# One layer's scan over 64 positions: one long scan instruction with reset columns, or sixteen short ones

## The chip, the cores and the metric

The kernel runs on one core of one Trainium2 chip. The metric is the device time of one launch in microseconds (us). Five engines work beside each other, each through its own queue of instructions in a fixed order: TensorE (PE, matmuls), VectorE (DVE), ScalarE (ACT), GpSimd (POOL) and SyncE (SP, which issues nearly all transfers here). An instruction whose operands are not ready stops everything behind it in its engine's queue.

## The reference, cut to what matters

A tensor of 32 images, 512 channels, 32 x 32 positions goes through four residual layers: x = x + layer(groupnorm(x)). Layer 0 weights channels by a spectrum, layer 1 is a grouped 3 x 3 convolution, layer 3 a deformable channel attention. Layer 2 is a three-level state-space model, and it is most of the work. At each level a feature map with 256 channels is read as a sequence of length L = 1024, 256 or 64, once forward and once backward, with 16 states per channel:

```python
dA  = jnp.exp(delta[..., None] * A)
dBx = delta[..., None] * Bs[:, :, None, :] * xt[..., None]
def step(h, inp):
    da, dbx, c = inp
    h = h * da + dbx
    return (h, jnp.einsum('bdn,bn->bd', h, c))
_, ys = lax.scan(step, h0, ...)          # h0 = 0
```

So each of the 256 x 16 pairs of channel and state has its own recurrence over the L positions, which starts from zero. At L = 64 and L = 256 both directions use the same weights and so the same dA and dBx; only the order of the positions differs. The output of a level is layer-normalised and added, doubled in both directions, to the next finer one.

## The kernel before, in words

**Tiles.** A tile for a scan has 128 partitions: 32 channels times 4 states. Its 1024 columns hold one sequence of 1024 positions (level "fine"), or four sequences of 256 (four groups of 32 channels, `nk` = 1), or sixteen sequences of 64 (four groups of channels times four groups of states, `nk` = 4). The function `fine` handles the level of 1024, the function `both` the levels of 256 and 64, with both directions in one call.

**One step of `both`.** PE spreads B over the partitions into PSUM (`pb`, L1548 at 64 positions, L1541 at 256). DVE multiplies it with delta times x (L1555). At 64 positions POOL forms the product delta times A (L1565) and ACT takes the exponential of all 1024 columns (L1580); at 256, ACT does both in four instructions (L1587). DVE scans (L1339 in the helper `scan`, called for r = 0 forward and r = 1 backward), POOL multiplies the result with C (L1625), PE sums over the states (L1635). An image has two halves of channels (d = 0, 1), so at 64 positions there are two exponentials, four scan steps (d, r) and four multiplications on POOL; in 32 images 64, 128 and 128.

**How sixteen sequences share one scan.** At 64 positions the scan instruction runs over all 1024 columns at once. So that no state passes from one sequence to the next, the factor dA in the first column of each sequence has to be zero. A tile `sv` (two buffers, cleared once at the start, L401) serves for this: ACT saves the first columns of `da` in `sv` (L1595) and overwrites them in `da` with zeros (L1599); the forward scan follows; before the backward scan one DVE reduction (L1606) puts the saved first columns back and zeros into the last ones. At 256 positions each of the four sequences already has a scan instruction of its own.

**The order of the work.** Every operation is recorded with an engine, an expected duration, its buffers and a key, a due time. `Plan.order` then replays the recording with the written durations: on each engine it starts, of the operations that are ready and have buffers, the one with the smallest key. What comes out is the instruction order of every engine; the chip only follows it. Keys count 100 units for an image. They are made of the constants at the head of the file: a place in the image for each stage (`FRONT`, `INPUTS`, `LOWER` and so on), shifts by image number (`PHASE`, `FIRST`, `FINAL`), and leads of single operations over their scan (the names ending in `_AHEAD`). `PE_RATE` multiplies the expected duration of every PE operation. Buffers are rings: `da` has 2, `pb` 2, `h` 6, `dt` 4.

**Fillers.** Where the replay leaves PE a gap of over 0.3 us while an accumulator (`y0`, `y1b`) is open, `between` puts matmuls of zeros into it (L1960), 0.8 of the gap by the written unit. `O_AHEAD` sets how early the accumulators are opened (L1364). These fillers add zero, and are real PE work.

Of the kernel before, what the change touches and what calls it, by code (L numbers as in the profile page):

```python
# [8 lines left out]
F32 = mybir.dt.float32  # L9
BF16 = mybir.dt.bfloat16  # L10
AF = mybir.ActivationFunctionType
ALU = mybir.AluOpType

P = 128
# [14 lines left out]
GROUP = 4  # L29
UNITS = 84  # L30

FRONT = (26.98339, 66.33591)
INPUTS = (97.00668, 120.78633)
Z = (73.71537, 86.62189)
DOWN = 115.11838
LOWER = (12.88324, 31.62883)
FINE1 = (22.72857, 46.22736)
FINE0 = (49.76984, 76.03085)
OUTPUT = (111.60985, 122.08898)
BACK = (68.71162, 156.12354)  # L40
SPECTRA = (57.12973, 128.4)

Z_0 = -72.5918
DOWN_0 = -124.07672
LOWER_0 = (-42.64059, -49.8751)
FRONT_E = (47.56605, -25.53413)
INPUTS_E = 6.96675
LOWER_E = (28.33012, 26.10135)
EVACUATE = 122.43595
LN_LATE = 10.7188  # L50
B_AHEAD, A_AHEAD, L_AHEAD, DB_AHEAD = 5.41553, 5.18574, 14.39657, 1.31239
C_AHEAD, Y_AHEAD, F_AHEAD, E_AHEAD = 5.20433, 0.75794, 9.0321, 4.34074
CC_AHEAD, CL_AHEAD, CA_AHEAD, CP_AHEAD = 7.94514, 17.86118, 5.24806, 5.3979
CB_AHEAD, CD_AHEAD = 5.83962, 1.9145
PE_RATE = 0.91418
O_AHEAD = 14.25035


class Buf:
# [175 lines left out]
def between(order):  # L235
# [21 lines left out]
KEEP_MIN, KEEP_SHARE, KEEP_UNIT = 0.3, 0.8, 0.213  # L257
STAGES = ("FRONT", "INPUTS", "DOWN", "LOWER", "FINE1", "FINE0", "OUTPUT", "BACK", "SPECTRA", "WEIGHTS")
PHASE = {
    "FRONT": (1.73998, -0.70898, 2.43732, -0.46783),  # L260
    "INPUTS": (-0.34062, 3.48827, 7.42205, -0.7684),
    "DOWN": (-0.28454, -1.33532, -2.28645, 10.95771),
    "LOWER": (-4.21848, 4.12408, 4.547, 2.27219),
    "FINE1": (-4.94045, -6.76105, 4.24822, 8.46924),
    "FINE0": (1.01816, -1.50111, 1.92083, 9.0252),
    "OUTPUT": (-3.45079, 6.79797, -9.49065, 1.76105),
    "BACK": (2.71819, 0.18102, 6.35319, -8.65591),
    "SPECTRA": (0.07386, 2.29523, -2.67145, -0.1361),
    "WEIGHTS": (4.55431, 2.37816, -5.2352, -47.942),
}  # L270
FIRST = {
    "FRONT": (-29.02061, -15.58957, -4.59773, 10.57713, -17.5828, -1.10449, -1.89262, -0.79223, 1.77484, 0.04765),
    "INPUTS": (5.35602, 0.39704, -1.54139, -3.11792, 3.98507, -25.36453, -4.27892, -2.71805, -3.56424, -9.18247),
    "DOWN": (-18.15189, -3.37029, 10.3643, -17.2826, -7.72621, 2.2188),
    "LOWER": (15.04982, 7.33067, 0.38748, -32.74476, -1.53709, 23.9531),
    "FINE1": (-27.62561, 15.94068, 40.70755, 4.75357, -13.35547, -3.68556),
    "FINE0": (-6.26626, -4.07582, 6.02046, -24.18655, 15.14066, -24.66011),
    "OUTPUT": (0.91761, 10.28771, 13.93866, -20.22127, -6.40573, 7.16333, -28.29682, -3.02744),
    "BACK": (-4.97178, 23.91988, 26.10169, 50.03687, -23.23641, 9.05568, -3.72902, 3.44514),
    "SPECTRA": (-36.87069, -17.04888, -4.24826, -12.25783, 7.70159, 8.04977, 2.40985, -5.14477, 4.98738, -5.21155, -0.54739, -3.88386, 0.27824, -2.0242),  # L280
    "WEIGHTS": (33.69103, -28.68007, 55.07658, 8.03152, 17.55966, 20.12364, -26.01811, -30.12737, -3.71784, 3.05174, 43.2247, -27.22466, -3.82396, -0.9483),
}
FINAL = {
    "FRONT": (-0.73596, -24.67755, -6.33942),
    "INPUTS": (-4.79937, 4.31975, 19.83127),
    "DOWN": (-5.09233, 3.22121, 21.47571),
    "LOWER": (-36.96369, 38.20998, 11.9625),
    "FINE1": (9.75884, -9.86524, 57.70702),
    "FINE0": (6.03965, 18.64503, -9.54717),
    "OUTPUT": (18.40436, -3.78191, 3.95094),  # L290
    "BACK": (49.74549, 3.63925, 12.96738),
    "SPECTRA": (2.96786, -20.64168, 8.41789),
    "WEIGHTS": (-20.80319, 27.97236, -51.95186),
}
T_DMA = 0.42
T_TABLE = 1.3
# [21 lines left out]
def kernel(ctx: ExitStack, tc: tile.TileContext, t: dict, out: bass.AP):  # L318
    nc = tc.nc
# [29 lines left out]
        "sbm": ([96, 256], BF16, 1, True),  # L349
        "sbc": ([96, 64], BF16, 1, True),  # L350
        "dg": ([P, P], F32, 1, True),
        "sv": ([P, 16, 2], F32, 2, True),
        "dt": ([P, 2, HW], F32, 4, True),
        "cb": ([P, HW], F32, 2, True),
        "da": ([P, HW], F32, 2, True),
# [41 lines left out]
    tiles = {}  # L397
    for n, (shape, dt, count, _) in shapes.items():
        tiles[n] = [const.tile(shape, dt, name=f"{n}{i}") for i in range(count)]
    for w in tiles["sv"]:  # L400
        nc.gpsimd.memset(w, 0.0)  # L401

    h_all = const.tile([P, H_TILES * HW], F32, name="h_all")
    tiles["h"] = [h_all[:, i * HW : (i + 1) * HW] for i in range(H_TILES)]
# [26 lines left out]
    for i in (1, 2, 3):  # L431
# [3 lines left out]
        w = const.tile([P, 2, P], F32, name=f"xw{i}")  # L435
        nc.gpsimd.memset(w, 0.0)
        r = slice((0, 80, 112, 120)[i], (0, 80, 112, 120)[i] + RDT)
# [41 lines left out]
    pl = Plan(rings)  # L479
# [19 lines left out]
    def act(fn, n, r, w, key, ptr=False, acq=()):  # L499
        return pl.op("ACT", t_act(n, ptr), fn, r, w, key, acq)  # L500

    def dve(fn, n, r, w, key, acq=()):
        return pl.op("DVE", t_dve(n), fn, r, w, key, acq)
# [833 lines left out]
    def scan(h, da, db, rev):  # L1337
        v = [z[:, ::-1] if rev else z for z in (h, da, db)]
        nc.vector.tensor_tensor_scan(v[0], v[1], v[2], 0.0, ALU.mult, ALU.add)  # L1339
# [156 lines left out]
    def both(lv, f, pre, ysum, below, n, ck):  # L1496
# [4 lines left out]
        nk = HW // (4 * n)  # L1501
# [16 lines left out]
        def pieces(z):  # L1518
            return z.rearrange("p (k q l) -> p k q l", k=nk, q=4)

        o = [P, nk, 4, n]
        for d in range(2):
# [11 lines left out]
            for k0 in range(0, 4, nk):  # L1534
                pb = pl.buf("pb")
# [26 lines left out]
                if nk > 1:  # L1562
# [7 lines left out]
                        ),  # L1570
                        HW, [(dt, 1)], [pr], ck.key(CP_AHEAD),
                    )
                da, sv = pl.buf("da"), nk > 1 and pl.buf("sv")

                def ends(da=da):
                    return pieces(da.t).rearrange("p k q l -> p (k q) l")

                if nk > 1:
                    act(
# [3 lines left out]
                else:  # L1583
                    for q in range(4):
# [5 lines left out]
                            ),  # L1590
                            n, [(dt, 1)], [(da, q)], ck.key(CA_AHEAD), True,
                        )
                if nk > 1:
                    act(
                        lambda sv=sv, ends=ends: nc.scalar.copy(sv.t[:, 0 : 4 * nk, 0:1], ends()[:, :, 0:1]),  # L1595
                        4 * nk, [da], [sv], ck.key(CA_AHEAD),
                    )
                    act(
                        lambda sv=sv, ends=ends: nc.scalar.copy(ends()[:, :, 0:1], sv.t[:, 0 : 4 * nk, 1:2]),  # L1599
                        4 * nk, [sv], [da], ck.key(CA_AHEAD),  # L1600
                    )
                for r in range(2):
                    h = pl.buf("h")
                    if r and nk > 1:
                        dve(
                            lambda sv=sv, ends=ends: nc.vector.tensor_reduce(  # L1606
                                ends()[:, :, 0 : n : n - 1],
                                sv.t[:, 0 : 4 * nk, :].rearrange("p k (e o) -> p k e o", o=1),
                                axis=mybir.AxisListType.X, op=ALU.max,
                            ),  # L1610
                            8 * nk + 60, [sv], [da], ck.key(),
                        )
                    if nk > 1:
                        pl.op(
                            "DVE", 2.21, lambda h=h, da=da, pb=pb, r=r: scan(h.t, da.t, pb.t, r == 1),
                            [da, pb], [h], ck.key(),
                        )
                    else:
                        def scans(h=h, da=da, pb=pb, r=r):
                            for q in range(4):  # L1620
                                scan(*(pieces(z.t)[:, 0, q, :] for z in (h, da, pb)), r == 1)

                        pl.op("DVE", 2.36, scans, [da, pb], [h], ck.key())
                    pool(
                        lambda h=h, k0=k0: nc.gpsimd.tensor_mul(  # L1625
                            pieces(h.t), pieces(h.t),
                            cbv()[:, k0 : k0 + nk, :].rearrange("p k (o l) -> p k o l", o=1).to_broadcast(o),
                        ),
                        HW, [h, cb], [h], ck.key(),
                    )  # L1630

                    def add(h=h, r=r, k0=k0, d=d):
                        for k in range(nk):
                            for q in range(4):
                                nc.tensor.matmul(  # L1635
                                    accv(r)[q * 32 : (q + 1) * 32, d, 0:n], lhsT=sel_y,
                                    rhs=pieces(h.t)[:, k, q, :],
                                    start=False, stop=False,
                                )

                    pe(add, 0.6 if nk == 1 else 0.69, [h], [acc[r]], ck.key(Y_AHEAD))
                    ck.u += 1
# [210 lines left out]
    while b < B:  # L1853
        n = min(1 if b < 2 else 2 if b < 4 else GROUP, B - b)
# [30 lines left out]
    def begin(b):  # L1885
# [4 lines left out]
        if b == 0:  # L1890
            m = moved("FRONT", 0)
            front(b, st[b], -340.0 + m, -310.0 + m)
# [31 lines left out]
    for b in range(B):  # L1924
# [6 lines left out]
        if own:  # L1931
            k = LOWER_E if b else LOWER_0
# [20 lines left out]
    with tc.manual_schedule():  # L1953
        for o in order:
# [3 lines left out]
            n, b, lo = spare.get(o, (0, None, 0))  # L1958
# [96 lines left out]
```

## Time and profile before

| | before |
|---|---|
| median of 3 runs | 10725.92 us (10714.02 to 10737.91) |
| the profiled execution's own time | 10725.94 us |
| its span, first to last instruction | 10723.8 us |
| PE busy | 9886.2 us, 92% (of it fillers L1960: 1478.3 us) |
| DVE busy | 9543.4 us, 89% |
| POOL busy | 8335.1 us, 78% |
| ACT busy | 7440.7 us, 69% |
| transfers | 191 GB/s, 71% of the DMA engines' time |
| granted PE clock | 0.972 |

Busy time counts an engine's overlapped instructions once. A group's "mean" is the length of one instruction from its start to its end, which can be longer than the distance to the next one: where busy time divided by the count is smaller than the mean, instructions overlap. PE's busy time holds the fillers, so that it says little on how near PE is to its limit. "Idle before" is the time an engine stood still just before the instructions of a group.

### The profile page before, as it was taken

The numbers are of one execution on the slowest core, as the hardware profiler recorded it, in microseconds if no ns is written. First come the engines' busy times: TensorE is split into PE (matmuls) and PEld (weight loads), VectorE is DVE, ScalarE is ACT, GpSimd is POOL, SyncE is SP. The second block draws the span as 40 slices with busy tenths as digits, with TensorE's granted clock in tenths as the row PEclk, the third lists the DMA queues.
The fourth block names the chain that finished last, engine by engine and source line by source line (L and its number), as shares of the span: only waits on it lengthen the run. The fifth ranks groups of instructions, "written<-read, shape, count | busy, mean of one in ns | idle before, by whom it ended". The sixth has DMA issues, their size and how long they took to land. (4 is left out here: it accounts for less than half of the span.)

```text
span 10723.8 us, 163029 instructions
## 1 busy us (share of the span) xinstructions
PE 9886.2 (92%) x55995; PEld 4522.1 (42%) x55995; DVE 9543.4 (89%) x9224; ACT 7440.7 (69%) x12932; POOL 8335.1 (78%) x5681
## 2 busy tenths in 40 slices
PE   8999999999999999999999999999999999999987
PEld 5454544434444444344443444434444434333333
DVE  2977878999999999999899998999999999999996
ACT  5677776776777767777777767777677776666654
POOL 2766677788788788887788878888877888878886
PEclk9999999999999999999999999999999999999999
DMA  5677667777877777777777767777777777776654
GB/s 170 163 193 193 178 178 197 193 185 203 217 197 188 196 194 206 210 194 198 193 208 196 199 186 205 197 197 204 196 209 198 189 196 190 202 205 185 166 139 134
DMA packets 897107, 2050.26 MB, mean 191 GB/s; under 512 B 230802, under 2 KB 363178, under 8 KB 883850
## 3 DMA queue, kind: packets, MB, share of 16 engines
q1 hardware_dynamic: 896256, 2039.74, 71.0%
q8 instruction: 442, 7.24, 0.3%
q14 instruction: 391, 3.20, 0.1%
q10 hardware_dynamic: 18, 0.09, 0.0%
HBM read 1609.80 MB, written 429.52 MB: 190 GB/s over the span
## 5 line engine op out<-in xcount | busy, mean ns | idle before, releaser
L1339 DVE TENSOR_TENSOR_SCAN h_all<-da,pb 128x1024 f32<-128x1024 f32 (+1 forms) x4224 | 6125.6, 1493 | 329.5 <-ACT da L1416 118.9
L1430 POOL TENSOR_TENSOR h_all<-h_all,cb 128x1024 f32<-128x1024 f32 x2048 | 4814.8, 2362 | 1582.4 <-DVE h_all L1339 1040.5
L1416 ACT ACTIVATE da<-dt,w_Al 128x1024 f32<-128x1024 f32 x2048 | 2335.9, 1147 | 1480.6 <-DVE h_all L1339 1069.5
L1422 DVE TENSOR_TENSOR pb<-dt,pb 128x1024 f32<-128x1024 f32 x2048 | 2446.1, 1215 | 265.8 <-PE pb L1409 171.7
L1625 POOL TENSOR_TENSOR h_all<-h_all,cb 128x1024 f32<-128x1024 f32 x640 | 1505.7, 2363 | 181.2 <-DVE h_all L1339 103.1
L1409 PE MATMUL pb<-sb,sel_b 96*128 96x512 bf16 x4096 | 1248.5, 387 | 369.6 <-DVE h_all L1339 297.9
L1960 PE MATMUL y<-sel_b,none_b 96*128 96x512 bf16 x5564 | 1478.3, 389 | 5.2 <-DVE sel_b L593 5.2
L1045 PE MATMUL mm<-x,wt 128*128 128x512 f32 x2048 | 981.0, 601 | 17.8 <-ACT x L565 4.0
L1409 PEld LDWEIGHTS <-sel_b 96*128 96x128 bf16 x4096 | 387.3, 102 | 1333.6 <-issue 1253.2
L1960 PEld LDWEIGHTS <-none_b 96*128 96x128 bf16 x5603 | 541.3, 103 | 755.5 <-issue 287.6
L992 PE MATMUL mm<-pk,wk 99*32 99x512 f32 (+1 forms) x6024 | 792.5, 607 | 42.1 <-DMA pk<-in_xp 27.4
L1438 PE MATMUL y<-h_all,w_sel_y 128*32 128x512 f32 x4096 | 615.4, 625 | 1.5 <-POOL h_all L1430 1.4
L710 PE MATMUL mm<-w_dct,sx 128*128 128x128 f32 x3968 | 565.7, 291 | 32.9 <-ACT sx L701 8.0
L710 PEld LDWEIGHTS mm<-w_dct,sx 128*128 128x128 f32 x3968 | 506.2, 199 | 185.7 <-ACT sx L701 42.9
L1438 PE MATMUL y1b<-h_all,w_sel_y 128*32 128x512 f32 x4096 | 569.8, 609 | 0.0
L1045 PEld LDWEIGHTS mm<-x,wt 128*128 128x128 f32 x2048 | 369.7, 189 | 422.1 <-issue 281.1
L1045 PE MATMUL mm<-y,w_out_w 128*128 128x512 f32 x1024 | 514.0, 616 | 15.6 <-ACT g L1715 2.7
L1587 ACT ACTIVATE da<-dt,w_Al 128x256 f32<-128x256 f32 x1024 | 464.0, 503 | 39.5 <-DVE h_all L1339 34.9
L1555 DVE TENSOR_TENSOR pb<-dt,pb 128x1024 f32<-128x1024 f32 x320 | 386.1, 1213 | 72.0 <-PE pb L1541 60.7
L1242 POOL TENSOR_TENSOR g<-g,f 128x512 f32<-128x512 f32 (+2 forms) x384 | 386.7, 1020 | 35.5 <-ACT g L1231 33.5
L1269 PE MATMUL mm<-ln,ones_d 128*128 128x512 f32 (+1 forms) x768 | 392.0, 599 | 20.2 <-ACT f L1075 8.3
L1192 PE MATMUL mm<-xd,dtw 64*128 64x512 f32 (+2 forms) x768 | 363.5, 560 | 35.4 <-DVE xd L1164 7.8
(286 smaller groups left out, 14556.5 us busy)
## 6 DMA issues: line engine op xcount, KB each, us to landing
dt<-dd SPq DMA_DIRECT2D x2048, 256.0 KB, 7.7
pk<-in_xp SPq DMA_DIRECT2D x753, 297.0 KB, 5.8
cb<-cd SPq DMA_DIRECT2D x1536, 128.0 KB, 3.7
dd<-g SPq DMA_DIRECT2D x256, 512.0 KB, 6.4
xr<-x SPq DMA_DIRECT2D x128, 512.0 KB, 6.8
yv<-fs SPq DMA_DIRECT2D x128, 512.0 KB, 5.0
dt<-ddm SPq DMA_DIRECT2D x512, 128.0 KB, 3.4
sx<-in_x SPq DMA_DIRECT2D x124, 512.0 KB, 5.3
```

Of the source, the lines that this page charges most:

```text
L710: nc.tensor.matmul(ps.t[:, j * P : (j + 1) * P], lhsT=sx.t[:, 1, i : i + P], rhs=dct, start=True, stop=True,)
L992: nc.tensor.matmul(ps.t[32 * q : 32 * q + 32, r0 * IMG : r1 * IMG].rearrange("p (r k) -> p r k", k=IMG), lhsT=wk.t[:, q, 32 * dy : 32 * dy ...
L1045: nc.tensor.matmul(ps.t, lhsT=w(k)[:, m * P : (m + 1) * P], rhs=r()[:, cols], start=(k == 0 and not opened), stop=(k == len(rhs) - 1),)
L1339: nc.vector.tensor_tensor_scan(v[0], v[1], v[2], 0.0, ALU.mult, ALU.add)
L1409: nc.tensor.matmul(pb.t[:, cols], lhsT=sel_b[:, k, :], rhs=sb.t[:, cols], start=True, stop=True,)
L1416: lambda da=da, z=dt[q], k=k, g=g: nc.scalar.activation(da.t, z.t[:, 1, :], AF.Exp, scale=A[lv][:, k, g : g + 1]),
L1422: lambda pb=pb, z=dt[q]: nc.vector.tensor_mul(pb.t, z.t[:, 0, :], pb.t), HW,
L1430: lambda h=h, cb=cb: nc.gpsimd.tensor_mul(h.t, h.t, cb.t), HW, [h, cb], [h],
L1438: nc.tensor.matmul(acc[i].t[q * 32 : (q + 1) * 32, :], lhsT=sel_y, rhs=hs[q].t[:, cols], start=False, stop=False,)
L1587: lambda da=da, quads=quads, q=q, g=g, k0=k0: nc.scalar.activation(pieces(da.t)[:, 0, q, :], quads(1)[:, q, :], AF.Exp, scale=A[lv][:, k0, ...
L1625: lambda h=h, k0=k0: nc.gpsimd.tensor_mul(pieces(h.t), pieces(h.t), cbv()[:, k0 : k0 + nk, :].rearrange("p k (o l) -> p k o l", o=1).to_br ...
L1960: nc.tensor.matmul(b.t[:, lo : lo + b.kept], lhsT=none_b, rhs=flat(sel_b)[:, 0 : b.kept], start=False, stop=False)
```

## The change

The tile `sv`, its clearing, the two ACT copies and the DVE reduction are gone. At 64 positions each scan step issues sixteen scan instructions of 64 columns, one for each sequence, where it issued one of 1024; the two scan steps of a half now use the same unchanged `da`. The written duration of the step is 3.15 in place of 2.21. Besides, nearly every constant of the order has another value: all stage places, all shifts by image, all leads, and `PE_RATE`.

```diff
-LOWER = (12.88324, 31.62883)
+LOWER = (13.513, 28.96824)
...
-CC_AHEAD, CL_AHEAD, CA_AHEAD, CP_AHEAD = 7.94514, 17.86118, 5.24806, 5.3979
-CB_AHEAD, CD_AHEAD = 5.83962, 1.9145
-PE_RATE = 0.91418
-O_AHEAD = 14.25035
+CC_AHEAD, CL_AHEAD, CA_AHEAD, CP_AHEAD = 7.47032, 19.39182, 5.02592, 5.90281
+CB_AHEAD, CD_AHEAD = 5.58549, 1.69698
+PE_RATE = 0.87173
+O_AHEAD = 22.13866
...
-        "sv": ([P, 16, 2], F32, 2, True),
...
-    for w in tiles["sv"]:
-        nc.gpsimd.memset(w, 0.0)
...
-                da, sv = pl.buf("da"), nk > 1 and pl.buf("sv")
-
-                def ends(da=da):
-                    return pieces(da.t).rearrange("p k q l -> p (k q) l")
+                da = pl.buf("da")
...
-                if nk > 1:
-                    act(
-                        lambda sv=sv, ends=ends: nc.scalar.copy(sv.t[:, 0 : 4 * nk, 0:1], ends()[:, :, 0:1]),
-                        4 * nk, [da], [sv], ck.key(CA_AHEAD),
-                    )
-                    act(
-                        lambda sv=sv, ends=ends: nc.scalar.copy(ends()[:, :, 0:1], sv.t[:, 0 : 4 * nk, 1:2]),
-                        4 * nk, [sv], [da], ck.key(CA_AHEAD),
-                    )
                 for r in range(2):
                     h = pl.buf("h")
-                    if r and nk > 1:
-                        dve(
-                            lambda sv=sv, ends=ends: nc.vector.tensor_reduce(
-                                ends()[:, :, 0 : n : n - 1],
-                                sv.t[:, 0 : 4 * nk, :].rearrange("p k (e o) -> p k e o", o=1),
-                                axis=mybir.AxisListType.X, op=ALU.max,
-                            ),
-                            8 * nk + 60, [sv], [da], ck.key(),
-                        )
-                    if nk > 1:
-                        pl.op(
-                            "DVE", 2.21, lambda h=h, da=da, pb=pb, r=r: scan(h.t, da.t, pb.t, r == 1),
-                            [da, pb], [h], ck.key(),
-                        )
-                    else:
-                        def scans(h=h, da=da, pb=pb, r=r):
+
+                    def scans(h=h, da=da, pb=pb, r=r):
+                        for k in range(nk):
                             for q in range(4):
-                                scan(*(pieces(z.t)[:, 0, q, :] for z in (h, da, pb)), r == 1)
-
-                        pl.op("DVE", 2.36, scans, [da, pb], [h], ck.key())
+                                scan(*(pieces(z.t)[:, k, q, :] for z in (h, da, pb)), r == 1)
+
+                    pl.op("DVE", 2.36 if nk == 1 else 3.15, scans, [da, pb], [h], ck.key())
```

More of the change, by code (lines that the diff above doesn't have):

```diff
@@ L30 @@
 UNITS = 84
[L32 to L35, printed above, removed]
-LOWER = (12.88324, 31.62883)
[L37 to L52, printed above, removed]
-CC_AHEAD, CL_AHEAD, CA_AHEAD, CP_AHEAD = 7.94514, 17.86118, 5.24806, 5.3979
-CB_AHEAD, CD_AHEAD = 5.83962, 1.9145
-PE_RATE = 0.91418
-O_AHEAD = 14.25035
+FRONT = (27.31004, 67.02807)
+INPUTS = (93.94834, 125.04711)
+Z = (74.67623, 81.77805)
+DOWN = 114.77346
+LOWER = (13.513, 28.96824)
+FINE1 = (23.19548, 47.21091)
+FINE0 = (51.35358, 78.96264)
+OUTPUT = (111.95446, 118.11289)
+BACK = (55.5241, 161.03937)
+SPECTRA = (54.70856, 128.30351)
+Z_0 = -105.07863
+DOWN_0 = -220.95057
+LOWER_0 = (-29.86063, -34.61059)
+FRONT_E = (48.91459, 3.04387)
+INPUTS_E = 9.5435
+LOWER_E = (29.80023, 7.07295)
+EVACUATE = 133.23714
+LN_LATE = 10.8511
+B_AHEAD, A_AHEAD, L_AHEAD, DB_AHEAD = 5.37078, 5.10994, 14.35379, 1.62967
+C_AHEAD, Y_AHEAD, F_AHEAD, E_AHEAD = 6.56594, 0.57586, 8.98335, 5.19642
+CC_AHEAD, CL_AHEAD, CA_AHEAD, CP_AHEAD = 7.47032, 19.39182, 5.02592, 5.90281
+CB_AHEAD, CD_AHEAD = 5.58549, 1.69698
+PE_RATE = 0.87173
+O_AHEAD = 22.13866
 class Buf:
@@ L259 @@
 PHASE = {
[L260 to L269, printed above, removed]
+    "FRONT": (4.73761, -0.28903, 5.77875, -0.61673),
@@ L270 @@
+    "INPUTS": (-5.30511, 2.65734, 5.73485, -0.37277),
+    "DOWN": (6.25453, -0.83769, -3.93846, 12.43911),
+    "LOWER": (-3.28637, 3.5377, 4.35329, 0.76018),
+    "FINE1": (-3.7777, -7.32571, 7.73012, 9.46184),
+    "FINE0": (-2.66305, -5.3351, -1.25818, 7.73328),
+    "OUTPUT": (-1.17514, 4.15285, -0.39845, 1.58054),
+    "BACK": (7.14305, -7.8301, 10.47171, -7.42362),
+    "SPECTRA": (0.05649, 2.36357, -2.74389, -0.17737),
+    "WEIGHTS": (4.03052, -12.29821, -8.33443, -45.10858),
 }
 FIRST = {
-    "FRONT": (-29.02061, -15.58957, -4.59773, 10.57713, -17.5828, -1.10449, -1.89262, -0.79223, 1.77484, 0.04765),
@@ L273 @@
[L273 to L278, printed above, removed]
@@ L279 @@
-    "BACK": (-4.97178, 23.91988, 26.10169, 50.03687, -23.23641, 9.05568, -3.72902, 3.44514),
-    "SPECTRA": (-36.87069, -17.04888, -4.24826, -12.25783, 7.70159, 8.04977, 2.40985, -5.14477, 4.98738, -5.21155, -0.54739, -3.88386, 0.27824, -2.0242),
-    "WEIGHTS": (33.69103, -28.68007, 55.07658, 8.03152, 17.55966, 20.12364, -26.01811, -30.12737, -3.71784, 3.05174, 43.2247, -27.22466, -3.82396, -0.9483),
+    "FRONT": (-27.52564, 11.14284, -15.05171, 30.02941, -23.32033, -15.87875, -12.07511, -2.96433, 0.9052, -2.73885),
@@ new lines @@
+    "INPUTS": (32.98002, 24.43932, 14.72288, 5.28944, -5.64191, -22.2843, -24.62038, -3.24191, -10.37639, -7.01109),
+    "DOWN": (-21.56508, -10.93218, 11.5105, -24.24021, -21.3927, 12.70338),
+    "LOWER": (34.01591, 10.32587, -4.47171, -25.48991, -0.66856, 21.58012),
+    "FINE1": (-32.26982, 15.66706, 32.27702, 7.15662, -39.90577, -0.34393),
+    "FINE0": (-3.26079, -9.71483, 21.02106, -24.35115, 19.72641, -26.05953),
+    "OUTPUT": (5.45725, 12.33286, 15.60198, -35.96714, -5.3198, 6.13576, -12.72858, -2.34173),
@@ L282 @@
+    "BACK": (-10.08665, 8.28069, 39.62304, 42.64832, -26.4346, -13.8819, -30.40457, -0.78097),
+    "SPECTRA": (-50.89355, -28.32336, -14.82804, -14.45231, 31.14369, 15.55765, 5.72886, -2.17973, 35.40677, -21.2843, -0.54779, -0.93164, -1.76293, -3.42053),
+    "WEIGHTS": (32.4412, -30.83669, 71.89057, 8.90844, 26.65968, 4.84071, -42.77211, -78.41173, -6.62991, 12.28345, 64.52262, -31.64528, 0.33291, 7.3203),
 }
 FINAL = {
-    "FRONT": (-0.73596, -24.67755, -6.33942),
-    "INPUTS": (-4.79937, 4.31975, 19.83127),
@@ L286 @@
[L286 to L293, printed above, removed]
+    "FRONT": (27.443, -32.26499, -6.70537),
+    "INPUTS": (-7.67726, -4.99709, 2.73194),
+    "DOWN": (4.51104, -6.37409, 79.88748),
@@ L294 @@
+    "LOWER": (-33.40447, 53.58347, 29.60236),
+    "FINE1": (12.63865, -13.89714, 82.8607),
+    "FINE0": (-5.19006, 1.7855, 9.26835),
+    "OUTPUT": (35.93553, 21.8516, 7.85491),
+    "BACK": (41.20561, -6.17039, 8.64673),
+    "SPECTRA": (-3.41341, -2.3044, 9.3649),
+    "WEIGHTS": (5.14431, 61.44699, -79.7461),
 }
```

## The prediction

> **What bounds the kernel now.** First the groups by line on DVE, with shapes kept apart. Behind the bar stand busy time and the mean length of one; then the idle time just before the group and what ended it.
>
> ```profile
> L1339 DVE TENSOR_TENSOR_SCAN h_all<-da,pb 128x1024 f32<-128x1024 f32 x2176 | 4908.9, 2275 | 326.9 <-ACT da L1416 118.9 <-PE y1b L1438 74.4 <-ACT da L1599 55.5
> L1339 DVE TENSOR_TENSOR_SCAN h_all<-da,pb 128x256 f32<-128x256 f32 x2048 | 1220.4, 661 | 2.6 <-issue 1.1 <-ACT da L1587 0.7
> L1606 DVE TENSOR_REDUCE da<-sv 128x32 f32<-128x32 f32 x64 | 13.2, 207 | 1.3
> ```
>
> Two thirds of DVE's busy time is scans. Of the 2176 long ones, 128 belong to the level of 64, the rest to the finest one. The last name in the first row is a wait that this change bears on: 55.5 us in which a scan waited for the copy that clears first columns.
>
> Then busy time by stretch (us, then PE, PE weight loads, DVE, ACT, POOL, then clock, DMA share, GB/s).
>
> ```profile
> 0.00:150.00 150.00, 124.07 (x778) 86.47 (x779) 20.43 (x82) 64.51 (x169) 21.86 (x64) 0.87 0.67 191
> ...
> 2400.00:5000.00 2600.00, 2413.24 (x13760) 1096.39 (x13760) 2430.01 (x2338) 1888.52 (x3277) 2117.49 (x1434) 0.98 0.75 201
> 5000.00:9800.00 4800.00, 4455.75 (x25218) 2000.26 (x25217) 4447.32 (x4181) 3384.42 (x5821) 3901.66 (x2641) 0.97 0.74 197
> ```
>
> From 2400 us on DVE works 93% of the time, ACT 71 to 73%, POOL 81%. PE's 93% contains the fillers, so DVE is the engine that sets the pace. Over the whole span DVE stands still 10723.8 - 9543.4 = 1180 us: about 206 before 300 us, 313 from there to 2000, 576 from there to 10300, 85 after that. So about 890 us of idle lie in the body, and a DVE microsecond is worth close to one of span.
>
> Third, a stretch with one image's step at 64 positions, on DVE in order of time (start, length).
>
> ```profile
> 4832.78 2.29 DVE L1339 TENSOR_TENSOR_SCAN h_all<-da,pb 128x1024 f32<-128x1024 f32 x1
> 4834.99 0.13 DVE L552 TENSOR_SCALAR sms<-mm 128x1 f32<-128x1 f32 x1
> 4835.11 0.21 DVE L1606 TENSOR_REDUCE da<-sv 128x32 f32<-128x32 f32 x1
> 4835.42 2.29 DVE L1339 TENSOR_TENSOR_SCAN h_all<-da,pb 128x1024 f32<-128x1024 f32 x1
> ...
> 4840.41 2.29 DVE L1339 TENSOR_TENSOR_SCAN h_all<-da,pb 128x1024 f32<-128x1024 f32 x1 [0.70 <-PE y1b L1438]
> 4842.73 0.21 DVE L1606 TENSOR_REDUCE da<-sv 128x32 f32<-128x32 f32 x1
> 4843.08 4.60 DVE L1339 TENSOR_TENSOR_SCAN h_all<-da,pb 128x1024 f32<-128x1024 f32 x5
> ...
> 4848.71 7.03 DVE L1339 TENSOR_TENSOR_SCAN h_all<-da,pb 128x256 f32<-128x256 f32 x12
> 4855.66 1.21 DVE L1555 TENSOR_TENSOR pb<-dt,pb 128x1024 f32<-128x1024 f32 x1
> ```
>
> Prices come from start to start, since neighbours overlap. A long scan: 4834.99 - 4832.78 = 2.21 here, 2.19 where the next instruction was ready early. Twelve short ones: 4855.66 - 4848.71 = 6.95, so 0.58 for one of 256. The reduction: 4835.42 - 4835.11 = 0.31 and 4843.08 - 4842.73 = 0.35.
>
> Fourth, ACT in the same stretch:
>
> ```profile
> 4837.83 1.06 ACT L1580 ACTIVATE da<-da 128x1024 f32<-128x1024 f32 x1 [0.19 <-DVE h_all L1339]
> ...
> 4839.33 0.20 ACT L1595 COPY sv<-da 128x16 f32<-128x16 f32 x1
> 4839.44 0.51 ACT L1587 ACTIVATE da<-dt,w_Al 128x256 f32<-128x256 f32 x1
> 4839.85 0.20 ACT L1599 COPY da<-sv 128x16 f32<-128x16 f32 x1
> ```
>
> The exponential is done at 4838.89, but `da` may be scanned only after 4840.05. The 0.70 us wait at 4840.41 is put down to PE; these copies ended last among the scan's own operands.
>
> **The change part by part.** The sum is made against the profiled execution, 10725.94 us, which equals the median of the runs (10725.92).
>
> *Sixteen scans for one.* From 256 to 1024 columns the price rises by 2.19 - 0.58 = 1.61 us, or 2.10 ns a column. For 64 columns that gives 0.58 - 192 x 0.0021 = 0.178 us, sixteen take 2.85, and a step gets 0.66 longer; 128 steps: +84 us. Upper end: no overlap, so 0.661 - 0.403 = 0.258 each, 4.13 a step, +248 us. I take the overlapped value, because the twelve short scans did overlap. The fixed part is then 0.178 - 0.134 = 0.044 us an instruction.
>
> [...] The row above gives 84, and the sum goes by the row.
>
> *The reduction goes.* 64 x 0.33 = -21 us on DVE. With the scans: +63.
>
> *Two copies fewer on ACT.* 13.6 + 13.9 = 27 us of an engine that is 69% busy count nothing by themselves. What counts is the chain: the scan may start 0.46 us earlier (4832.24 to 4832.70 in the first half) or 1.16 us (4838.89 to 4840.05). Ends for the 27 waits of 55.5 us in all: 27 x 0.46 = 12, and all 55. I take the mean, 27 x 0.81 = -22. What is late next is the exponential itself, behind POOL's product (L1565, 1.90 us).
>
> *Who waits longer.* POOL's multiplication by C (L1625) waits for the sixteenth piece, 0.66 us later; behind it in POOL's queue stand the finest level's multiplications, which have six `h` buffers of slack. ACT's next exponential into the same `da` waits for the second scan: 2 x 0.66 - 0.33 = 1 us later, with one other buffer as cover. These delays are DVE time already counted if DVE sets the pace. If POOL does: in this stage (4830 to 4848 us) POOL was busy 17.68 of 18 us and DVE 16.25. POOL's share of an image there is 2 x 1.90 + 4 x 2.36 = 13.2 us; DVE's is 2 x 1.15 + 4 x 2.19 + 2 x 0.33 = 11.7 before, 13.7 after. Paced by POOL, the stage grows by 0.5 and not 2.0 us an image: 16 us instead of 63. I take 63, because outside this stage POOL has slack to catch up and DVE has little.
>
> *The order anew.* In the order of the two built programs SP issues the same 7806 instructions, and POOL's and ACT's other work keeps its counts. Counted with row durations, the ACT work ahead of the exponential of the 64th, 512th and 1536th scan of the finest level differs by at most 30 us (380, 2365, 6456 before; 379, 2360, 6426 after), POOL's by at most 5. So stages stay in place and only neighbours swap. Long stretches without an exponential on ACT (over 7 us of other work) are 112 before, 105 after. I see no gain large enough to count, and cost the swaps at nothing; cover is the rings, and if they run dry DVE's body idle of 890 us grows or shrinks (rival 1).
>
> *Fillers.* Their count rises from 5603 to 6825, by 22%. At 1478.3 / 5564 = 0.266 us, PE gets 325 us more work, against 838 us in which it now stands still. DVE's waits for what PE spreads into `pb` are these:
>
> ```profile
> DVE pb L1422 <- PE pb L1409: 171.7, 177, 4.6
> ...
> DVE pb L1555 <- PE pb L1541: 60.7, 41, 7.9
> ```
>
> If they grow with the fillers: 232 x 0.22 = +51 us. The other end is 0, all fillers in time that PE waits anyway. I take 15, nearer to 0 because the replay put them into gaps.
>
> Sum: 84 - 21 - 22 + 15 = +56, so **10782 us**. Own range of this case: from 16 - 22 = -6 (POOL paces, fillers free), 10720, to 84 - 21 - 12 + 51 = +102, 10828.
>
> **Rivals.**
>
> 1. *The new offsets take away waits* (faster). For it: 890 us of body idle, with waits of many small kinds, which offsets can move. Against it: order statistics that hardly differ. It decides once more than 41 + 15 = 56 us, or 6% of the 890, go. At 15%: -133, so 10726 + 56 - 133 = 10649 us; I give it 10600 to 10705. [...]
>
> 2. *PE becomes the bound through fillers* (slower). PE's share would be (9886 + 325) / 10782 = 95%. If a third of the 325 delays DVE, 108 in place of 15: 10875 us. Against it: PE stands still mostly because DVE holds `pb` (297.9 us of waits at L1409).
>
> 3. *Short scans do not overlap* (slower): 248 - 21 - 22 + 15 = +220, 10946 us. Against it: the twelve above.
>
> That the change does not do what it says is excluded: the built program has 128 steps of sixteen 64-column scans and no reduction.
>
> **How the numbers follow.** Forecast case 0.46, rival 1 0.38, rival 2 0.10, rival 3 0.06. A measurement of this kernel tells about 0.2%, 21 us. Faster: 0.36 of rival 1 and 0.01 of the forecast case, 0.37. Same: 0.08 of the forecast case, 0.02 of rival 1, 0.10. Slower: 0.37 + 0.10 + 0.06 = 0.53. The range from 10625 to 10885 leaves out the lowest quarter of rival 1 (0.09), the upper part of rival 2 (0.04) and rival 3 (0.06). The forecast case alone has 10720 to 10828.
>
> **What would show it.** Right: 2048 scans of 64 columns with about 365 us of busy time; DVE busy near 9610; no wait on an L1599; body idle near 870. Body idle below 830 speaks for rival 1. Waits of `pb` multiplications for PE above 280 us speak for rival 2; 64-column scans with over 0.2 us of busy time each for rival 3. The prediction is wrong if the swaps matter, since the trace of before cannot price them.

## The result and the profile after

The changed kernel takes 10851.44 us (median of 4 runs, 10833.22 to 10867.11), the kernel before 10723.52 us in the same comparison. The ratio is 1.0115, with a 95% interval from 1.01 to 1.0129: some 125 us slower, where +56 was forecast. The profiled execution, the fastest of the four, took 10833.22 us, with a span of 10831.4.

First the page's busy times of the changed kernel, then its groups by line on DVE, shapes kept apart (busy, mean ns of one; idle before and what ended it). Lines of the unchanged code stand 3 to 28 numbers lower than before.

```profile
PE 10114.8 (93%) x57217; PEld 4625.7 (43%) x57217; DVE 9604.5 (89%) x11080; ACT 7438.1 (69%) x12804; POOL 8339.8 (77%) x5679
```

```profile
L1336 DVE TENSOR_TENSOR_SCAN h_all<-da,pb 128x1024 f32<-128x1024 f32 x2048 | 4612.1, 2274 | 234.4 <-ACT da L1413 145.4 <-PE y1b L1435 40.7 <-issue 6.6
...
L1336 DVE TENSOR_TENSOR_SCAN h_all<-da,pb 128x256 f32<-128x256 f32 x2048 | 1220.1, 663 | 4.6 <-ACT da L1581 3.8
...
L1336 DVE TENSOR_TENSOR_SCAN h_all<-da,pb 128x64 f32<-128x64 f32 x2048 | 373.2, 260 | 27.8 <-ACT da L1574 19.7 <-PE y L1435 4.0 <-ACT sg L540 3.9
```

The 2048 short scans (the "pieces" below) take 373.2 us, 0.182 each; the forecast had 0.178. DVE's busy time rose from 9543.4 to 9604.5, +61, where scans and reduction together were forecast at +63. Nothing is wrong with these prices. But DVE's idle time rose too, from 1180 to 10831.4 - 9604.5 = 1227 us, +47. In the body, from 300 to 10300 us, it is 926 us, where the forecast expected the 890 of before to fall to 870.

The step at 64 positions in an image in the middle (DVE, in order of time):

```profile
4882.89 2.33 DVE L1552 TENSOR_TENSOR pb<-dt,pb 128x1024 f32<-128x1024 f32 x2
4885.13 2.94 DVE L1336 TENSOR_TENSOR_SCAN h_all<-da,pb 128x64 f32<-128x64 f32 x16
4887.99 0.66 DVE L1161 TENSOR_TENSOR xd<-mm,sb 64x512 f32<-64x512 f32 x1
4888.58 2.93 DVE L1336 TENSOR_TENSOR_SCAN h_all<-da,pb 128x64 f32<-128x64 f32 x16
...
4892.19 1.23 DVE L1552 TENSOR_TENSOR pb<-dt,pb 128x1024 f32<-128x1024 f32 x1 [0.58 <-PE pb L1538]
4893.39 2.96 DVE L1336 TENSOR_TENSOR_SCAN h_all<-da,pb 128x64 f32<-128x64 f32 x16
4896.26 0.13 DVE L539 TENSOR_TENSOR sms<-sms,mm 128x1 f32<-128x1 f32 x1
4896.31 2.95 DVE L1336 TENSOR_TENSOR_SCAN h_all<-da,pb 128x64 f32<-128x64 f32 x16
4903.56 0.16 DVE L549 TENSOR_SCALAR sms<-mm 128x1 f32<-128x1 f32 x1 [4.31 <-PE mm L546]
4903.67 2.42 DVE L1336 TENSOR_TENSOR_SCAN h_all<-da,pb 128x256 f32<-128x256 f32 x4
```

Sixteen pieces run without a gap, 2.86 us from start to start. The long stop comes afterwards: an instruction on one column (L549, 0.16 us) waits 4.31 us for PE and holds up the next scans behind it: they start at 4903.67, though their own exponentials (L1581) were done at 4895.58.

Who made DVE wait, before and then after (us in total, times, longest):

```profile
DVE pb L1422 <- PE pb L1409: 171.7, 177, 4.6
...
DVE sms L756 <- POOL sms L750: 76.9, 14, 24.3
...
DVE h_all L1339 <- ACT da L1599: 55.5, 27, 5.6
...
DVE sms L552 <- PE mm L549: 42.1, 18, 4.8
...
DVE sms L542 <- PE mm L539: 37.6, 22, 10.0
```

```profile
DVE pb L1419 <- PE pb L1406: 142.6, 144, 4.5
...
DVE sms L753 <- POOL sms L747: 95.3, 22, 24.0
DVE pb L1552 <- PE pb L1538: 80.8, 59, 6.6
...
DVE sms L549 <- PE mm L546: 58.7, 21, 12.0
...
DVE sms L539 <- PE mm L536: 54.6, 24, 8.6
...
DVE yc L1277 <- PE mm L1266: 25.4, 11, 5.2
```

The wait for the copy (L1599) is gone. PE keeps `pb` waiting slightly less in all: with the row of 60.7 us in the prediction the two waits make 232.4 us before, and 223.4 after (less at the finest level, more at the level of 256). That is no sign of rival 2, which was to show above 280. What else grew are waits in front of small instructions of dependent chains: the statistics of the spectra, `sms`, in these three rows by 52 us, and the layer norm of the level of 64, `yc`, 25.4 us, for which DVE's groups by line had 5.6 before.

When the time is lost can be read by lining up the 2048 multiplications by C of the finest level on POOL (L1430 before, L1427 after), 64 an image, which come in the same number: the start of each is compared with the start of the same one in the kernel before. The after kernel is 7 us ahead at the 224th, 48 us behind at the 256th, and from there falls back to 108 us behind at the 2048th, some 2 us an image, though unevenly: 34 of these 60 us come between the 1536th and the 1792nd. The step of 55 us at the start is a longer hole on DVE:

```profile
1572.27 0.14 DVE L678 TENSOR_SCALAR sms<-sg 128x1 f32<-128x1 f32 x1
...
1648.31 0.22 DVE L1161 TENSOR_TENSOR xd<-mm,sbc 64x64 f32<-64x64 f32 x1 [4.39 <-ACT sbc L1159]
...
1669.98 1.23 DVE L1552 TENSOR_TENSOR pb<-dt,pb 128x1024 f32<-128x1024 f32 x1 [3.96 <-DMA dt<-ddc]
...
1675.77 4.38 DVE L1336 TENSOR_TENSOR_SCAN h_all<-da,pb 128x64 f32<-128x64 f32 x24 [0.60 <-ACT da L1574]
```

Between 1572 and 1670 us no scan and no multiplication for one runs. The kernel before has a hole at the same work:

```profile
1600.62 0.22 DVE L1164 TENSOR_TENSOR xd<-mm,sbc 64x64 f32<-64x64 f32 x1 [2.30 <-ACT sbc L1162]
...
1627.80 2.29 DVE L1339 TENSOR_TENSOR_SCAN h_all<-da,pb 128x1024 f32<-128x1024 f32 x1 [2.04 <-ACT da L1599]
```

There the input of the 64-position level (`xd` from `sbc`) is formed at 1600.62, not 1648.31, and the first scan starts at 1627.80, not 1675.77: 48 us earlier both times. Both constants and code differ between the two kernels, so that this alone does not tell which of the two makes the difference.

### The profile page after: what moved, and what is told of

Same layout as the page of the kernel before. It is cut to its first block, busy times and chain, and to the rows that moved or that the text cites. A ratio compares the mean times of both kernels' runs of the same rounds, so it can differ in the third digit from the quotient of the medians.

```text
span 10831.4 us, 167209 instructions
## 1 busy us (share of the span) xinstructions
PE 10114.8 (93%) x57217; PEld 4625.7 (43%) x57217; DVE 9604.5 (89%) x11080; ACT 7438.1 (69%) x12804; POOL 8339.8 (77%) x5679
## 5 line engine op out<-in xcount | busy, mean ns | idle before, releaser
L1336 DVE TENSOR_TENSOR_SCAN h_all<-da,pb 128x1024 f32<-128x1024 f32 (+2 forms) x6144 | 6202.6, 1066 | 266.9 <-ACT da L1413 145.4
L1427 POOL TENSOR_TENSOR h_all<-h_all,cb 128x1024 f32<-128x1024 f32 x2048 | 4815.5, 2365 | 1608.9 <-DVE h_all L1336 1079.5
L1932 PE MATMUL y<-sel_b,none_b 96*128 96x512 bf16 x6761 | 1777.7, 388 | 0.0
L1932 PEld LDWEIGHTS <-none_b 96*128 96x128 bf16 x6825 | 656.9, 102 | 948.5 <-issue 370.6
L1581 ACT ACTIVATE da<-dt,w_Al 128x256 f32<-128x256 f32 x1024 | 462.4, 501 | 28.5 <-DVE h_all L1336 25.3
L1064 PE MATMUL mm<-f,wt 128*128 128x256 f32 (+1 forms) x1984 | 377.0, 329 | 6.0 <-ACT wk L945 1.9
```

What stands on the lines that cost most here:

```text
L1427: lambda h=h, cb=cb: nc.gpsimd.tensor_mul(h.t, h.t, cb.t), HW, [h, cb], [h],
L1581: lambda da=da, quads=quads, q=q, g=g, k0=k0: nc.scalar.activation(pieces(da.t)[:, 0, q, :], quads(1)[:, q, :], AF.Exp, scale=A[lv][:, k0, ...
L1932: nc.tensor.matmul(b.t[:, lo : lo + b.kept], lhsT=none_b, rhs=flat(sel_b)[:, 0 : b.kept], start=False, stop=False)
```

## The experiments

Each ratio is to the kernel before on the same chip, with its 95% interval.

**First question: the pieces or the order?** Three theories: the pieces cost the 61 us of DVE time that they add and the order the rest; the 1222 further fillers cost the rest; or the pieces cost everything through waits behind them.

*Pieces in the old order.* What the planner sees is left as it was; only what is issued differs.

```diff
-  lambda ...: nc.scalar.copy(sv.t[...], ends()[:, :, 0:1]),     # and the second copy
-  lambda ...: nc.vector.tensor_reduce(...),
+  lambda: None,
...
-  pl.op("DVE", 2.21, lambda ...: scan(h.t, da.t, pb.t, r == 1), ...)
+  pl.op("DVE", 2.21, sixteen, ...)        # sixteen scans of 64 columns
```

> The order of the kernel before, instruction for instruction, with its constants and fillers; only the scan step at 64 positions is sixteen scans of 64 columns, and the two copies and the reduction are not emitted. Theory 1 (the pieces cost what they add to DVE's busy time, the rest of the +125 us comes with the new order): about 60 us over the kernel before, 10785, with DVE busy near 9605 and its body idle as before. Theory 2 (the rest comes from the 1222 further fillers on PE): the same, 10785. Theory 3 (waits behind the sixteenth piece double the price of the pieces): about 10845. The forecast's own terms (scans +84, reduction -21, shorter chain -22) give 10765.

Measured: 10729.55 us, ratio 0.9995 (0.9985 to 1.0006). No theory had this: in the old order the pieces are free, to within the interval of -16 to +6 us.

```profile
PE 9874.3 (92%) x55995; PEld 4524.4 (42%) x55995; DVE 9609.0 (90%) x11080; ACT 7434.1 (69%) x12804; POOL 8341.9 (78%) x5681
```

DVE works 65.6 us more than in the kernel before, and the span is 3.9 us shorter: its idle time fell from 1180 to 1111.

*Long scans in the new order.*

```diff
 nc.scalar.activation(da.t, pr.t, AF.Exp)
+nc.scalar.copy(saved()[:, 0 : 4 * nk, 0:1], ends()[:, :, 0:1])
+nc.scalar.copy(ends()[:, :, 0:1], saved()[:, 0 : 4 * nk, 1:2])
...
+if r: nc.vector.tensor_reduce(...)
+scan(h.t, da.t, pb.t, r == 1)            # in place of the sixteen
```

> The order of the changed kernel with its constants and fillers, but at 64 positions one long scan again, with the two copies straight behind the exponential and the reduction straight ahead of the backward scan. Theory 1: the changed kernel less 60 us, 10790, so still 65 us over the kernel before, and the hole on DVE around 1570 to 1670 us still there. Theory 2: also about 10790. Theory 3: about 10725, as the kernel before.

Measured: 10864.74 us, 1.0122 (1.0104 to 1.014). No theory had this time either. It is the changed kernel's ratio (1.0115) without the pieces. So the loss lies in the new order, its fillers included.

```profile
PE 10117.0 (93%) x57217; PEld 4628.1 (43%) x57217; DVE 9538.5 (88%) x9224; ACT 7458.7 (69%) x12932; POOL 8332.7 (77%) x5681
```

The mirror image: DVE works 66 us less than in the changed kernel and stands still 76 us more (10841.6 - 9538.5 = 1303). The hole is there too, as theory 1 had it: its lag behind the kernel before grows from -1 us at the 224th multiplication to +59 at the 256th, and to 116 at the end.

*Fewer fillers.*

```diff
-KEEP_MIN, KEEP_SHARE, KEEP_UNIT = 0.3, 0.8, 0.213
+KEEP_MIN, KEEP_SHARE, KEEP_UNIT = 0.3, 0.66, 0.213
```

> The changed kernel with 0.66 in place of 0.8 of each gap filled: 5569 fillers in place of 6825, about as many as the kernel before has (5603); the order of all else is unchanged. Theory 1: 10850 within 15 us, since fillers lie in gaps. Theory 2: about 10790. Theory 3: 10850.

Measured: 10881.83 us, 1.0132 (1.0112 to 1.0152), against 1.0115 for the changed kernel: 30 us over what theories 1 and 3 expected, and not below, as theory 2 did. The granted clock of TensorE fell as well, from 0.969 to 0.961 (medians of the runs), so that this kernel changes two things; by their net effect, fewer fillers recover nothing. That the 1222 further fillers are not the loss is clearer from two kernels below, which lose 1.1% and 1.4% with 425 and 370 more than the kernel before, and from one that has 1307 more in the old order and loses nothing.

*Old constants, new code, planned anew.* All constants of the head of the file from before, the changed kernel's code with its 3.15.

> The changed kernel's code, step durations included, with all constants of the kernel before, so that the order is planned anew for the pieces but from the old due times. Theory 1: 10785, no hole of DVE around 1570 to 1670 us as long as in the changed kernel. Theory 2: fillers are 6214 here, half of the rise, so about 10815. Theory 3: 10850.

Measured: 10927.57 us, 1.0185 (1.0165 to 1.0204). This is worse than either kernel and than all three theories, though the old constants make the kernel before and the pieces have shown themselves free in its order. What is new in it is only the plan. The hole is not gone, though theory 1 expected that: the lag behind the kernel before grows from 18 us at the 224th multiplication to 75 at the 256th.

**Second question: why are the pieces free?**

*No reset at all*, long scans in the old order, the copies and the reduction not issued:

```diff
-  lambda ...: nc.scalar.copy(...),          # both copies
-  lambda ...: nc.vector.tensor_reduce(...),
+  lambda: None,
```

> The order of the kernel before with its long scans, but the two copies on ACT and the reduction on DVE are left out, so that state runs from one sequence into the next at 64 positions and the output is another one. Theory A (at this stage neither DVE nor the chain over ACT sets the pace, so the pieces were free): equal to the kernel before, 10733 within 20 us. Theory B (pieces cost about 60 us, and dropping copies and reduction gives about 60 back, which is why pieces in the old order came out equal): 10670.

Measured: 10732.81 us, 0.9998 (0.9989 to 1.0007). As theory A had it, dropping the reduction and the chain, which the forecast priced at 21 + 22 us, brings nothing.

*Pieces and reset together*, in the old order:

```diff
-  pl.op("DVE", 2.21, lambda ...: scan(h.t, da.t, pb.t, r == 1), ...)
+  pl.op("DVE", 2.21, sixteen, ...)          # copies and reduction stay
```

> The order of the kernel before with sixteen scans a step, and the two copies and the reduction kept, though the pieces no longer need them. Theory A: equal to the kernel before, 10733 within 20 us. Theory B: 80 us over it (128 steps times 0.66), 10815.

Measured: 10767.36 us, 1.0031 (1.0018 to 1.0043), +36 us by the medians. Neither theory: with the reset kept the pieces do cost something, less than half of the 84 us that DVE works more (9627.4 against 9543.4). This would fit some cover at this stage, which the pieces or the reset alone fit into and both together do not; no run measures that cover by itself.

```profile
PE 9895.1 (92%) x55995; PEld 4540.3 (42%) x55995; DVE 9627.4 (89%) x11144; ACT 7449.6 (69%) x12932; POOL 8337.3 (77%) x5681
```

*POOL relieved*, in the old order, once with long scans and once with pieces:

```diff
 nc.gpsimd.tensor_mul(
-    pieces(h.t), pieces(h.t), cbv()[:, k0 : k0 + nk, :]...
+    pieces(h.t)[:, 0:1], pieces(h.t)[:, 0:1], cbv()[:, k0 : k0 + 1, :]...   # 256 of 1024 columns, at 64 positions
```

> The order of the kernel before with its long scans; at 64 positions POOL multiplies only 256 of the 1024 columns of each scan result by C, so that the output is another one and POOL is relieved of some 1.65 us in each of 128 steps, 211 us in all. Theory A1 (POOL sets the pace of this stage, 13.2 us an image against DVE's 11.7): about 48 us below the kernel before, 10685. Theory A2 (nothing sets the pace here alone; rings and later catching up absorb small delays of any engine): within 20 us of the kernel before, 10733.

> The same relief of POOL (256 of 1024 columns multiplied, another output), with sixteen scans a step and no copies and no reduction, in the order of the kernel before. Theory A1: with POOL out of the way the pieces show their price, 60 us over the relieved kernel with long scans. Theory A2: equal to it within 20 us.

Measured: 10735.34 and 10739.46 us, both 1.0004 (0.9995 to 1.0013). POOL worked 207 and 215 us less than in the same orders unrelieved, and nothing got faster; the pieces stayed free. Theory A2 held: POOL does not set the pace here either.

Where the pieces' time goes can be followed step by step, because the kernel before and its copy with pieces have the same order. For the images 6 to 31 the start of each multiplication and scan step on DVE was compared in the two traces, and the lag just ahead of the stage taken off. The instruction behind the four scan steps starts about 0.7 us later with pieces (standard error 0.25). Four longer steps and two reductions fewer would make about 4 x 0.66 - 2 x 0.33 = 2.0. Ten operations on, 0.6 us are left, a hundred on 0.2, each with an error of 0.3. So about two thirds are made up inside the stage, and the rest is lost in the noise a hundred operations on. The waits by line go the same way: the 55.5 us for the cleared column become 22.9 for the exponential.

```profile
DVE h_all L1339 <- ACT da L1580: 22.9, 16, 3.5
```

**Third question: what does planning anew cost by itself?** These kernels execute the same instructions as the one before, fillers apart; one written number differs.

```diff
-"DVE", 2.21, lambda h=h, da=da, pb=pb, r=r: scan(h.t, da.t, pb.t, r == 1),
+"DVE", 3.15, lambda h=h, da=da, pb=pb, r=r: scan(h.t, da.t, pb.t, r == 1),     # 2.22 and 2.20 in two others
```

> The kernel before, executing the same instructions, but with 3.15 written for a scan step at 64 positions in place of 2.21, so that the order is planned anew from old constants. Theory C (an order is a fit to the chip, and any new planning loses it): 10840 to 10930. Theory D (only the new constants are to blame): 10735, and the 10928 of the changed code with old constants would come from something else in that code.

> The kernel before with 2.22 written for a scan step at 64 positions in place of 2.21: the same instructions executed, the same constants, planned anew; about half of DVE's instructions then stand at another place. Theory C (any new planning loses what the old constants were fitted to): 10790 to 10870, as with 3.15. Theory D (the loss grows with the change of the number): 10733 within 20 us.

> The kernel before with 2.20 written for a scan step at 64 positions in place of 2.21: the same instructions executed, planned anew. Theory C: 10790 to 10930, as with 2.22 (10891) and 3.15 (10853). If the direction of the number counts: at or below 10733.

Measured: 10853.16 us with 3.15, 1.0112 (1.0097 to 1.0126); 10890.98 with 2.22, 1.0141 (1.0128 to 1.0155); 10884.63 with 2.20, 1.0151 (1.0129 to 1.0172). A hundredth of a microsecond in a number that no engine ever sees costs more than 1%, upwards and downwards. Theory D is out; theory C named the direction, with 2.22 coming out 21 us above its range. With 2.22, 47% of the places in DVE's queue hold another instruction, from about the 225th on. In these three the size and the direction of the step in the number do not order the loss.

*New constants, old code.*

> The code of the kernel before (long scans, 2.21) with all constants of the changed kernel, planned anew. Theory C (constants fit only the one order they were found with): 10850 to 10940, no better than the old constants on the new code (10928). Theory E (the new constants are themselves the worse choice, by what the changed kernel lost): 10855. Theory F (they are good constants, spoilt by the pieces): 10735.

Measured: 10856.86 us, 1.0119 (1.0099 to 1.0139). Theory F is out. The time lies where theory E put it; but the three above, with the old constants, lie there as well, so it does not tell theory E from theory C.

*The changed kernel with one hundredth more.*

```diff
-pl.op("DVE", 2.36 if nk == 1 else 3.15, scans, [da, pb], [h], ck.key())
+pl.op("DVE", 2.36 if nk == 1 else 3.16, scans, [da, pb], [h], ck.key())
```

> The changed kernel with 3.16 written for a scan step at 64 positions in place of 3.15: the same instructions executed, planned anew. Theory C1 (its constants too were found by measuring exactly its order): 0.5 to 1.5% over the changed kernel, 10900 to 11010. Theory C2 (its order is an ordinary one, as any planning gives): 10850 within 60 us.

Measured: 10925.06 us, 1.0187 (1.0166 to 1.0209): 0.7% over the changed kernel, inside the range of theory C1. One neighbour does not tell a fit of the constants from chance.

**More fillers in the old order.** The old order with more of each gap filled (0.97 in place of 0.8):

> The kernel before with 0.97 in place of 0.8 of each gap filled: 6910 fillers in place of 5603, as the changed kernel has (6825), order of all else unchanged. If fillers delay PE (rival 2 of the forecast): above 10733, up to 10840. If they keep the granted clock up: clock above 0.973 and 10700 to 10725. If neither: 10733.

Measured: 10714.47 us, 0.9984 (0.9973 to 0.9996), with a granted clock of 0.9755 (median of the runs) against 0.971. It is the only one of sixteen kernels here whose interval lies below the one before, by 0.16%, and the interval ends at 0.9996: a thin gain. With pieces and still more fillers (1.1), two changes at once, it is gone:

> Sixteen scans a step in the order of the kernel before, with 1.1 in place of 0.8 of each gap filled: 7904 fillers in place of 5603. If fillers go on lifting the granted clock: clock near 0.98 and 10690 to 10715, below both kernels. If they begin to delay PE: 10740 or more.

Measured: 10738.06 us, 1.0007 (0.9998 to 1.0016), with a clock of 0.978, higher still. So this higher granted clock did not come with a shorter time; which of the two changes took the gain away was not separated.

## Why the prediction was right or wrong

The direction held, for the wrong reason: the size was missed by a factor of 2.2, and the forecast case's own range (10720 to 10828) did not hold 10851. Two steps failed. The new order was costed at nothing and costs about 125 us; the edit itself was costed at +41 us (84 - 21 - 22) and costs nothing in the old order. That +56 has the sign of the measured loss is luck, since no term of its sum is the one that made it.

*Sixteen scans for one.* Right as a price: 0.182 us a piece against 0.178, the overlap seen with 256 columns holds at 64 (a piece lasts 0.260 us, but sixteen take 2.86 from start to start, 0.179 each). Rival 3 is out. Of the fixed part the row had 0.044 us an instruction; 0.182 less 64 x 0.0021 leaves 0.048. With the reset kept, DVE's busy time rose by 84 us (from 9543.4 to 9627.4), the row's figure.

*What a DVE microsecond is worth.* This step failed: "a DVE microsecond is worth close to one of span". DVE was the busiest engine if PE's fillers are left out (9543.4 us against 9886.2 - 1478.3 = 8407.9), but in the old order 66 us more of its work added nothing. Of the 2.0 us an image that the steps should have cost, about 1.3 were made up inside the stage. Busy shares over thousands of microseconds could not show that.

*Reduction -21 and chain -22.* The wait did shrink, from 55.5 to 22.9 us. But taking reduction and chain away alone brought nothing, so that these terms were not worth their price either. The terms are not additive: 0 for pieces with the reset gone, 0 for the reset gone alone, 36 us for pieces with the reset kept.

*Who waits longer.* The forecast considered POOL as the pace of the stage, with +16 us. POOL relieved of over 200 us changed nothing, so that reading is out as well; that it came out nearest, with 16 - 22 = -6 us for the edit against a measured 0, is luck.

*The order anew.* This step failed too, and it is the term that decides: the forecast wrote "stages stay in place and only neighbours swap" and cost the swaps at nothing. Roughly they do: with DVE's instructions numbered by kind, half of them stand at most 2 places from where they stood and 95% at most 17, of some 290 an image; but a few moved by over 100. These moves cost about 125 us. The counts used (work ahead of a given exponential, long stretches without one) cannot see which instruction in a queue waits and stops the scans behind it, as L549 does for 4.31 us above. Rival 1 named the right mechanism, waits that offsets move, and expected only gains. With the pieces issued in both, DVE stands still in the body for 818 us in the old order and 926 in the new: 108 us more, 12% of the 890, where rival 1 reckoned with 15% less.

*Fillers.* No run supports the +15 us: more of them in the old order gave 0.16%, and fewer in the new order did not help. Rival 2 is out. Its counter-argument, that PE stands still "mostly" because DVE holds `pb`, overstates its row: 297.9 of 838 us are 36%.

**What the order costs, and what stays open.** Six plannings that differ from both kernels gave ratios of 1.0112, 1.0119, 1.0141, 1.0151, 1.0185 and 1.0187. The changed kernel's 1.0115 is at the low end of them; the kernel before, at 1, is far outside. So the change's cost is that an exceptionally good order was given up for one close to those that other numbers give. That the old constants were found by measuring this exact order would explain it; the runs show only that they do not survive a change of 0.01. The longer hole is a matter of the order and not of pieces or constants as such: between the 224th and the 256th multiplication the changed kernel loses 55 us, long scans in the new order 60, and old constants with new code 58, while the old code replanned with 3.15 gains 17 there (39 us behind, then 22). That one ends 112 us behind all the same, so the hole is one way to lose the time and not the reason that replanning loses it. For the remaining part, the grown waits in front of `sms` and `yc` go along with the loss; no run moved these instructions alone, so that they are its cause is argued and not shown. Nor is it shown what gives DVE its room at 64 positions, except that it is not POOL.

## What to carry to other kernels

Where a planner makes the order from tuned numbers, any edit that touches what it sees is two changes at once. Build the edit once inside the frozen order, and the old code once inside the new one; that separates them, and here these two kernels showed that the edit was free and the new order cost everything. Forecast such a change with the spread of orders (here 1.1 to 1.9% above the tuned one) rather than with the edit's own microseconds. And do not price an engine's added work by its share of busy time (89% for DVE here, and 66 us more of its work cost nothing in the old order); nor did the wait in front of it give the price here, since taking away the 55.5 us wait alone brought nothing.

## What the runs showed that was not expected

A number that only the planner reads, changed from 2.21 to 2.22, moved the device time by 1.4%. DVE, 89% busy, took 66 us more work in the old order without a longer span (10719.9 us against 10723.8). And 1307 more matmuls of zeros cost nothing on a PE that was 92% busy without them: the granted clock was 0.9755 in place of 0.971, and the kernel 0.16% shorter. That the clock made it shorter is not shown.
